# A transformer-like graph kernel in f32: one weight tile moved into the attention, one half of the layer norm's statistics moved behind the queries' products

## The chip, the cores and the metric

The kernel runs on one core of a Trainium2 chip. The metric is the device time of one execution, in microseconds (us). A core has five engines, which work side by side and wait for each other through semaphores: TensorE (PE in the profile) multiplies matrices into PSUM; VectorE (DVE) and ScalarE (ACT) do elementwise work; GpSimd (POOL) does a little of it and issues some transfers; SyncE (SP) issues most transfers. Each engine takes its own instructions strictly in the order in which the kernel wrote them.

## The reference, cut to what matters

`x` is 16 batches of 1024 nodes with 256 channels. Everything is f32.

```python
# layer 0
h = relu(layernorm(x))
c = mean of h over the channels              # one number a node
A = abs(abs(sigmoid(c_m - c_n) - 0.5) - 0.5) * 2, symmetrised
g = einsum('bcn,bnm->bcm', h^T, adj * A)     # graph sums
q = relu(g * para)^T                         # 4 heads of 64
k, v = split(h @ kv_w)
x = x + softmax(q k^T * scale) v
# layer 1
h = relu(layernorm(x))
agg = einsum('nm,bmd->bnd', A_hat, h)        # A_hat from adj
z = relu(batchnorm(agg @ W1.T + b1))
x = x + batchnorm(z @ W2.T + b2)
```

The weights `adj * A` are made from `1 - tanh(abs(c_m - c_n) / 2)`, for eight tiles of 128 nodes a batch.

## The kernel before

The batches are pipelined. While the attention of batch b runs, the weights of batch b+1 are begun. Then come the graph sums and the queries, keys and values of b+1 (`graph_seven`), then the first linear part of layer 1 of batch b (`linear1_all`), then the attention of b+1. One such cycle repeats for b = 1 to 14; batch 0 and 1 have a start of their own, and the last batches and the second linear layer with its batch norm stand at the end. Inside the main part the order of every engine is the order of the lines in the program (`manual_schedule`), so a step that is moved in the code moves in its engine's queue.

**The attention** (`attention`) has four steps for a batch, each for half of the queries and one pair of heads. `scores` (L797) makes eight tiles: PE multiplies keys by queries into one of three PSUM tiles of `ps_s` (L803), ACT takes the exp (L811), DVE adds the exps up (L817, L823, L826). Behind the eighth tile come the steps in `before_last` (L829), then the last addition (L831), then the steps in `after_last` (L832). `partial` turns and reduces the sums on DVE (L839, L847), `values` multiplies the exps by the values on PE (L855) and turns the result on DVE (L868). In the third step ACT also runs `collect` (L882) and `spread` (L897) for the first half's reciprocals.

**The weight tiles** are hung on these steps by `hooks` (run in `before_last`) and `aside` (run in `after_last`), L1449 to L1456. `differences` (L350) makes Abs (L353) and Tanh (L356) on ACT. What is left, subtracting one and multiplying by `adj`, is done in one of two ways: `masked` (L370) with one DVE instruction, or `masked_aside` (L359) with a small memset on DVE (L363), which ACT waits for, an Identity on ACT (L365) and a product on POOL (L366). `weights` (L344) is `differences` and `masked` together. Before, tiles 0 to 3 are made in steps 0 to 3 of the attention with `masked_aside`; tiles 4 to 7 are made in `graph_seven` with `masked`.

**The graph sums** (`graph_seven`, from L509) multiply a matrix of 2 x 2 blocks with seven products in place of eight (a Strassen form, in Winograd's order). The products `m1` to `m_7` go to PSUM: one accumulator `x` that ACT copies out three times (L631, L655, L659), `m7`, and the two tiles `gps[0]` and `gps[1]`. DVE makes the sums of weight tiles (`make_t1` to `make_t4`: L557, L560, L553, L565). At the end DVE joins the parts: L662, L673, L675 and L676 add PSUM to the copies in `room`; L667 to L671 make sums of `hT` for the keys and values.

**Values and keys** (`Seven`, from L684) have the same form of seven products each. All copies of the accumulator run on ACT (L727), all additions on DVE (L730), and products 6, 5 and 3 go on in the accumulator only after the copy ahead of them. The values' products are L717 on PE, the keys' L712. Between them stand the queries' products with `para` (L742), `add1` (the second half of the attention's result is added to `x`, L931), the store of `x` (`leave`) and the load of the next (`arrive`), both on SP's queue.

**The layer norm of layer 1** (`Norm`): `stats` is eight instructions for four node tiles (L253 four times, L255 four times, DVE), `invert` an addition on DVE (L259) and a power on POOL (L260), `shifts` one DVE instruction that waits for the power (L266), `relu` one ACT instruction a node tile (L281). Before, `stats`, `invert` and `shifts` of tiles 0 to 3 stand among the joining additions of the graph sums (L660, L661, L672), their relus among the values' products (L735, L740); those of tiles 4 to 7 stand behind `add1` (L752, L753, L762), with relus among the keys' products (L774, L779). The first products of the linear layer (L1018) read the relus of tiles 0 to 3.

POOL also issues half of the sixteen small transfers that lay out the attention's result (L923); SP issues the other half.

## Time and profile before

| | |
|---|---|
| median of 3 runs | 2389.51 us (2387.36 to 2390.91) |
| the profiled execution | 2388.5 us, its span 2386.6 us |
| instructions | 25696 |
| mean granted clock of TensorE | 0.995 |
| exps (L811, ACT) | 512, 477.4 us busy |
| scores (L803, PE) | 2048 records, 457.3 us busy |
| masks on DVE (L370) | 71, 84.0 us busy, 1217 ns each |
| masks on POOL (L366) | 56, 132.3 us busy, 2362 ns each |

The span is what the profiler saw from the first to the last instruction; the execution's own time has 1.9 us around it. A line of the timeline gives the start in us, the duration, the engine, the line of the kernel, the operation, the tiles written and read, the shapes and the count; in square brackets stand the idle time of the engine ahead of it and what ended it. PE's records overlap, since matmuls are pipelined, so their starts are read. One f32 matmul of 512 columns leaves two records. "V" below is the start of the first values' product of a cycle.

### The profile page before, as it was taken

Reading aid. Unit: us, or ns where it says so; the run is one execution under the profiler, and the core shown is the slowest. Engines: PE = TensorE matmul, PEld = TensorE weight load, DVE = VectorE, ACT = ScalarE, POOL = GpSimd, SP = SyncE. Lnnn points to the kernel's source line nnn. Section 1 sums busy time; section 2 is a strip of 40 time slices with the busy share of each in tenths; the row PEclk is TensorE's granted clock in tenths of the full one; section 3 lists DMA queues with packets and bytes.
Section 4 is the critical chain, followed back from the end, with each engine's and each line's share of the span. In section 5 each row is a group of like instructions: output and inputs, shape, how many; then the busy total and the mean of one; then the engine's idle time right before and its main releaser. Section 6 shows DMA issues by size and latency. Waiting matters only on the chain.

```text
span 2386.6 us, 25696 instructions
## 1 busy us (share of the span) xinstructions
PE 2341.1 (98%) x8258; PEld 1031.6 (43%) x8258; DVE 1977.9 (83%) x2922; ACT 1418.5 (59%) x2058; POOL 444.2 (19%) x565
## 2 busy tenths in 40 slices
PE   8999999999999999999999999999999999999995
PEld 4443444434343434444343434344443434444444
DVE  6888989897988889897979898897979798757766
ACT  6846556473847465565748375656656575446654
POOL 3041212122212112121122211121212121100000
PEclk9999999999999999999999999999999999999998
DMA  5043343523342434435233424243353421355569
GB/s 194 10 141 97 133 141 115 159 106 115 105 145 82 172 98 135 139 115 159 106 119 123 142 71 168 94 166 108 125 149 112 133 100 54 109 207 187 175 239 380
DMA packets 167264, 323.78 MB, mean 136 GB/s; under 512 B 33616, under 2 KB 100688, under 8 KB 167120
## 3 DMA queue, kind: packets, MB, share of 16 engines
q1 hardware_dynamic: 143696, 266.44, 32.7%
q0 software_dynamic: 18816, 38.83, 6.0%
q10 hardware_dynamic: 4608, 16.78, 1.7%
q8 instruction: 67, 1.10, 0.2%
q14 instruction: 77, 0.63, 0.1%
HBM read 202.38 MB, written 100.72 MB: 127 GB/s over the span
## 4 chain that ended last, share of the span: by engine, by line
PE 63%; DVE 20%; issue 6%; ACT 5%; POOL 4%; DMA 1%; DVEq 0%; SPq 0%; ACTq 0%; POOLq 0%
PE f_aps L1018 16%; PE f_s L803 11%; PE f_o L855 11%; PE f_zps L1125 6%; PE f_zx L1672 4%; ACT f_p L811 4%; PE f_zm L1672 3%; DVE f_w L370 3%; POOL f_att L923 2%; PE f_kpsx L712 2%; DVE f_w L557 2%; DVE f_sums L826 2%; PE f_kps L712 2%; DVE f_sums L839 1%; DVE f_v L553 1%
## 5 line engine op out<-in xcount | busy, mean ns | idle before, releaser
L811 ACT ACTIVATE f_p<-f_s 128x1024 f32<-128x1024 f32 x512 | 477.4, 1046 | 89.1 <-PE f_s L803 88.9
L803 PE MATMUL f_s<-f_qT,f_kT 64*128 64x512 f32 x2048 | 457.3, 596 | 0.5 <-issue 0.5
L855 PE MATMUL f_o<-f_p,f_v 128*64 128x512 f32 x2048 | 453.6, 595 | 0.0
L803 PEld LDWEIGHTS f_s<-f_qT,f_kT 64*128 64x128 f32 x2048 | 191.1, 186 | 264.2 <-issue 117.7
L855 PEld LDWEIGHTS f_o<-f_p,f_v 128*64 128x64 f32 x2048 | 141.4, 137 | 304.3 <-issue 265.1
L366 POOL TENSOR_TENSOR f_w<-f_w,f_adj 128x1024 f32<-128x1024 f32 x56 | 132.3, 2362 | 700.7 <-ACT f_w L365 565.2
L923 POOL DMA_DIRECT2D f_att<-f_oT x256 | 136.7, 541 | 398.3 <-DVE f_oT L906 391.4
L826 DVE TENSOR_TENSOR f_acc<-f_acc,f_p 128x1024 f32<-128x1024 f32 x128 | 155.9, 1218 | 4.5 <-ACT f_p L811 4.5
L826 DVE TENSOR_TENSOR f_sums<-f_sums,f_p 128x1024 f32<-128x1024 f32 x128 | 155.8, 1217 | 0.0
L353 ACT ACTIVATE f_w<-f_row,f_col 128x1024 f32<-128x1024 f32 x127 | 147.0, 1157 | 13.7 <-DMA f_row<-frow 10.3
L356 ACT ACTIVATE f_w<-f_w 128x1024 f32<-128x1024 f32 x127 | 134.4, 1058 | 4.0
L817 DVE TENSOR_TENSOR f_acc<-f_p,f_p 128x1024 f32<-128x1024 f32 x64 | 78.5, 1226 | 56.3 <-ACT f_p L811 56.3
L1018 PE MATMUL f_aps<-f_ahatT,f_hs 128*128 128x512 f32 x256 | 115.1, 592 | 0.0
L1018 PE MATMUL f_aps<-f_ahatT,f_h_b 128*128 128x512 f32 x256 | 112.7, 593 | 0.1
L1018 PE MATMUL f_aps<-f_t,f_hs 128*128 128x512 f32 x256 | 112.5, 592 | 0.0
L572 PE MATMUL f_gps<-f_w,f_h_a 128*128 128x512 f32 x224 | 111.0, 598 | 0.0
L365 ACT ACTIVATE f_w<-f_w,f_now 128x1024 f32<-128x1024 f32 x56 | 64.3, 1149 | 75.3 <-DVE f_now L363 75.2
L281 ACT ACTIVATE f_h_a<-f_x,f_shift_a,f_rstd_a 128x256 f32<-128x256 f32 x126 | 73.8, 587 | 37.2 <-DVE f_shift_a L266 37.2
L281 ACT ACTIVATE f_h_b<-f_x,f_shift_b,f_rstd_b 128x256 f32<-128x256 f32 x128 | 69.3, 595 | 43.9 <-DVE f_shift_b L266 43.9
L823 DVE TENSOR_TENSOR f_sums<-f_p,f_p 128x1024 f32<-128x1024 f32 x64 | 78.1, 1221 | 20.5 <-ACT f_p L811 20.4
L370 DVE SCALAR_TENSOR_TENSOR f_w<-f_w,f_adj 128x1024 f32<-128x1024 f32 x71 | 84.0, 1217 | 4.2 <-ACT f_w L356 4.2
L1148 ACT ACTIVATE f_z<-f_zps,f_b 128x512 f32<-128x512 f32 x60 | 38.0, 684 | 75.2 <-PE f_zps L1125 75.2
(292 smaller groups left out, 3982.6 us busy)
## 6 DMA issues: line engine op xcount, KB each, us to landing
f_t<-ft SPq DMA_DIRECT2D x84, 512.0 KB, 9.9
fz<-f_z SPq DMA_DIRECT2D x64, 512.0 KB, 9.8
f_x<-in_x_dram SPq DMA_DIRECT2D x31, 1024.0 KB, 7.9
f_zb<-fz SPq DMA_DIRECT2D x42, 512.0 KB, 4.6
fx<-f_x SPq DMA_DIRECT2D x16, 1024.0 KB, 4.4
fgs<-f_gs POOLq DMA_DIRECT2D x28, 512.0 KB, 3.0
fhT<-f_hQ POOLq DMA_DIRECT2D x112, 128.0 KB, 3.2
f_hT<-fhT SPq DMA_DIRECT2D x28, 512.0 KB, 6.3
```

What stands on the lines that cost most here:

```text
L281: nc.scalar.activation(self.h[:, c, :], self.xt[:, c, :], AF.Relu, bias=self.shift[:, c : c + 1], scale=self.rstd[:, c : c + 1], accum_out ...
L353: nc.scalar.activation(w, rows[b], AF.Abs, bias=cols[b][:, c : c + 1], scale=0.5 / C)
L356: nc.scalar.activation(w, w, AF.Tanh)
L370: nc.vector.scalar_tensor_tensor(w, w, 1.0, adj_t[c], ALU.subtract, ALU.mult)
L803: nc.tensor.matmul(ps[:, e, :], kT[rows_e, pair, ts(m, P)], qT[rows_e, pair, ts(g, 512)], start=True, stop=True,)
L811: nc.scalar.activation(p, ps, AF.Exp)
L826: nc.vector.tensor_add(to, to, p)
L855: nc.tensor.matmul(o_of[s][e * HD : (e + 1) * HD, :], v[:, m, ts(2 * pair + e, HD)], p[:, e, :], start=(m == 0), stop=(m == NC - 1),)
L923: queue.dma_start(t[ts(j, 32), :, a].rearrange("r h c i -> r h (c i)"), oT[ts(a, 32), :, j].rearrange("r h c i -> r h (c i)"),)
L1018: nc.tensor.matmul(ps, left[:, m, :], right(m), start=not more and m == 0, stop=(m == KH - 1), skip_group_check=more,)
L1125: nc.tensor.matmul(ps[i], left[:, ts(i, P)], right, start=not more, stop=True, skip_group_check=more,)
L1672: nc.tensor.matmul(ps, left[:, m, :], right[:, m, :], start=start and m == 0, stop=(m == 1), skip_group_check=not start,)
```

## The change

Three things are changed, in all fourteen cycles.

- Tiles 0, 2, 3 and 4 are made in steps 0 to 3 of the attention with `masked_aside`, and tile 1 in step 1 as well, with `weights`, whose DVE instruction stands ahead of L831. `graph_seven` makes tiles 5 to 7 only.
- `stats`, `invert` and `shifts` of the first half are moved from the end of the graph sums behind `add1`, around two of the values' additions; their four relus move from among the values' copies to among the keys' copies. The last addition from `gps[1]` (L676) moves ahead of the sums of `hT`.
- `gps[1]` is allocated ahead of `gps[0]`.

```diff
-            gps = [ps_s.tile([P, N], F32, tag="s", name=f"f_gps_{b}_{d}") for d in range(CC)]
+            gps = {
+                d: ps_s.tile([P, N], F32, tag="s", name=f"f_gps_{b}_{d}") for d in reversed(range(CC))
+            }
             add0, collect, invert, spread, scale, add1 = left
-            for c in range(4):
-                assert (b, c) in ws
-            w4th = w4.tile([P, N], F32, tag="w4", name=f"f_w_{b}_4")
...
-            differences(b, 4, w4th)
             differences(b, 5, w5th)
...
-            masked(b, 4)
             masked(b, 5)
...
             nc.scalar.copy(room[:, 1], x)
-            norm.stats(0, 4)
-            norm.invert(0, 4)
             nc.vector.tensor_add(room[:, 2], room[:, 2], m7)
+            nc.vector.tensor_add(room[:, 2], room[:, 2], gps[1][:, 0:512])
...
             nc.vector.tensor_sub(kt4, part(1, 0), kt2)
-            norm.shifts(0, 4)
             nc.vector.tensor_add(room[:, 3], room[:, 1], m7)
             both = lambda d: room[:, 2 * d : 2 * d + 2].rearrange("p n k -> p (n k)")
             nc.vector.tensor_add(both(0), both(0), gps[0])
-            nc.vector.tensor_add(room[:, 2], room[:, 2], gps[1][:, 0:512])
...
             V.copy(0, 0)
-            norm.relu(0, 2, False)
             V.product(2)
...
             V.copy(1, 0)
-            norm.relu(2, 4, False)
...
             load_more(2, 3)
+            norm.stats(0, 4)
+            norm.invert(0, 4)
             V.add(1, 0, 7)
             V.add(1, 1, 7)
+            norm.shifts(0, 4)
             norm.stats(4, NC)
             norm.invert(4, NC)
...
             K.copy(0, 0)
+            norm.relu(0, 2, False)
             K.product(2)
             norm.shifts(4, NC)
             K.add(0, 0, 2)
             K.product(6)
             K.copy(1, 0)
+            norm.relu(2, 4, False)
...
                 if b + 1 < B:
-                    for c in range(2 if b == 0 else 4):
-                        if b == 0:
+                    if b == 0:
+                        for c in range(2):
                             hooks.setdefault(c, []).append(lambda c=c: weights(b + 1, c))
-                            continue
-                        hooks.setdefault(c, []).append(lambda c=c: differences(b + 1, c))
-                        aside[c] = [lambda c=c: masked_aside(b + 1, c)]
+                    else:
+                        for i, c in enumerate((0, 2, 3, 4)):
+                            hooks.setdefault(i, []).append(lambda c=c: differences(b + 1, c))
+                            aside[i] = [lambda c=c: masked_aside(b + 1, c)]
+                        hooks[1].append(lambda: weights(b + 1, 1))
```

## The prediction, made before the changed kernel ran

> **What bounds the kernel now.** I read the page's busy times first, then the starts of the matmuls in order of time, then who waited for whom, then ACT, DVE and POOL in one cycle.

> ```profile
> PE 2341.1 (98%) x8258; PEld 1031.6 (43%) x8258; DVE 1977.9 (83%) x2922; ACT 1418.5 (59%) x2058; POOL 444.2 (19%) x565
> ```

> PE sets the time; a stall counts only where PE's next matmul starts late. The cycle of a batch lasts 130.2 to 130.3 us in 11 of the 13 full cycles (130.6 and 134.3 in the others), and the matmuls' starts cut it: graph sums 24.58, values' products 6.88, keys' products 6.31 (so 13.19 for both), linear layer 36.15, attention 56.34. A 512-column f32 matmul record follows the last after 0.429 us where nothing waits (linear layer: 56 records in 24.03). So the graph sums hold 0.55 us of waiting and the products about 1.1: more than that times 14 cycles can't be won there. What the engines beside PE do between the first product (806.51) and the linear layer (819.70):

> ```profile
> 804.61 0.68 DVE L662 TENSOR_TENSOR f_kT<-f_kT,f_gps 128x512 f32<-128x512 f32 x1
> 808.75 0.16 DVE L266 SCALAR_TENSOR_TENSOR f_shift_b<-f_mv_b,f_rstd_b 128x4 f32<-128x4 f32 x1 [0.93 <-POOL f_rstd_b L260]
> 808.83 0.68 DVE L673 TENSOR_TENSOR f_kT<-f_kT,f_gps 128x512 f32<-128x512 f32 x1
> 811.88 2.35 DVE L742 TENSOR_TENSOR f_qT<-f_kT,f_qT 128x1024 f32<-128x1024 f32 x2
> 814.15 1.22 DVE L931 TENSOR_TENSOR f_x<-f_x,f_att 128x1024 f32<-128x1024 f32 x1
> 815.29 1.28 DVE L730 TENSOR_TENSOR f_v<-f_v,f_vps 128x512 f32<-128x512 f32 x2
> 816.49 1.40 DVE L253 BATCH_NORM_STATS2 f_st_b<-f_x 128x6 f32<-128x256 f32 x4
> 817.80 0.36 DVE L255 BATCH_NORM_AGGREGATE f_mv_b<-f_st_b 128x2 f32<-128x6 f32 x4
> 818.20 0.17 DVE L259 TENSOR_SCALAR f_var_b<-f_mv_b 128x4 f32<-128x4 f32 x1
> 818.44 1.01 POOL L260 TENSOR_TENSOR f_rstd_b<-f_var_b,f_mhalf 128x4 f32<-128x4 f32 x1 [9.72 <-DVE f_var_b L259]
> 819.49 0.17 DVE L266 SCALAR_TENSOR_TENSOR f_shift_b<-f_mv_b,f_rstd_b 128x4 f32<-128x4 f32 x1 [0.53 <-POOL f_rstd_b L260]
> 819.69 1.09 ACT L281 ACTIVATE f_h_b<-f_x,f_shift_b,f_rstd_b 128x256 f32<-128x256 f32 x2 [1.00 <-DVE f_shift_b L266]
> ```

> DVE is one unbroken row of work here; the first shifts (808.75) wait for POOL. From the end of the statistics' additions (L259, 818.20) it takes 1.29 us through POOL to the shifts, and 0.20 more to the relu. PE's keys hang on ACT's copies:

> ```profile
> 816.30 0.59 ACT L727 COPY f_kT<-f_kpsx 128x512 f32<-128x512 f32 x1 [1.22 <-PE f_kpsx L712]
> 816.96 1.10 PE L712 MATMUL f_kpsx<-f_hT,f_kvs 128*128 128x512 f32 x2
> ```

> Copy start to next product start: 0.66.

> **Part one: the first half's statistics go behind the queries' products.** Out of the graph sums' end go four L253, four L255, L259, the wait for POOL and L266. They come back after L931, but the relus that need the shifts now stand in ACT's queue *ahead* of the keys' copies: copy, relu 0-1, copy, relu 2-3. Count from the first values' product (V = 806.51). DVE, start to start as in the rows: L662 starts when the copy L655 is done, V-3.5; L676 (moved up) 0.70 later, since it adds to the same tile; the four hT sums end at V+0.4. L673 waits for the copy L659 (0.20 to 0.79): V+0.85, where it stood at V+2.32. L675 0.72 later; 1.14 for it; 0.60 for V.add; L742 twice 1.13; L931 1.14; with 0.06 for the dependence the statistics start at V+6.78. L253 1.32, L255 0.40, L259 0.08, then two V.adds. POOL's power starts 0.25 after L259 (V+8.50) and takes 1.01; shifts at V+9.79; relu at V+9.99. The pair of relus holds ACT 1.00 us (808.95 to 809.95 before), so the second keys' copy starts at V+10.99 and the product behind it at V+11.65. Before it stood at 816.96 = V+10.45: **1.20 us later**. From there to the linear layer it is 2.74 as before: relu 2-3 ends before the next copy's data (1.14 after the product), so it is hidden, and the relus 4-5 stand behind the third copy with shifts ready by V+13.1.
> What the values win ahead of that is eaten: L673 frees the bank of product 7 at V+1.5 (before: V+3.0, PE stood 0.36), and copy (1,0) no longer stands behind two relus (809.95), so the keys' products start near V+6.5 instead of V+6.88; but PE then stands some 1.5 us at the fifth product. Bounds: 0.9 (DVE gaps of 0.60 where I took 0.70 to 1.14 for two of them, and no relu overhead) to 1.45 (POOL's power at the 1.24 of the first half's row, L260 at 807.48). I take 1.20. POOL has nothing else at that time: its eight attention issues ran 803.20 to 807.47. SP sees its store of x1 behind L931 some 2 us sooner, which nothing waits for.

> There is one gift. In the fourth cycle the values' products took 10.92 instead of 6.88: POOL's issues of f_att paused for 2.65 us, the power came late, L266 with DVE behind it 3.39 late, and PE stood 2.63. After the change the power is asked for at V+8.5, so such a pause is covered: **-4.0 us once** (0 if the pause falls elsewhere).

> [...]

> **Part two: the fifth weight tile in the attention.** The graph sums lose an Abs, a Tanh and a masked product (L370, 1.13 apart). Two of their products wait for L370 (0.09 and 0.27 us beyond 0.429), both behind three L370 in a row; with one fewer both masks are ready in time: **-0.36** (bounds 0 and -0.55, all the waiting there). In exchange the second attention step gets Abs, Tanh and L370 of tile 1. The rows of that step and the next:

> ```profile
> 879.60 1.06 ACT L356 ACTIVATE f_w<-f_w 128x1024 f32<-128x1024 f32 x1
> 882.05 1.15 ACT L365 ACTIVATE f_w<-f_w,f_now 128x1024 f32<-128x1024 f32 x1 [1.40 <-DVE f_now L363]
> 885.19 5.61 ACT L811 ACTIVATE f_p<-f_s 128x1024 f32<-128x1024 f32 x6 [1.99 <-PE f_s L803]
> 880.71 1.22 DVE L831 TENSOR_TENSOR f_acc<-f_acc,f_sums 128x1024 f32<-128x1024 f32 x1
> 881.88 0.06 DVE L363 MEMSET f_now<- 128x1 f32 x1
> 884.02 7.14 PE L803 MATMUL f_s<-f_qT,f_kT 64*128 64x512 f32 x32
> ```

> ACT seems to have room (1.40 + 1.99 idle against 2.2 of work), but the room is cut up by DVE. Tanh of tile 2 ends at 880.66, so tile 1's Abs and Tanh end at 882.9. L370 stands in DVE's queue ahead of L831 and the memset, and waits for that Tanh: 882.93; L831 1.14 later, 884.07; memset 1.17 later, 885.24; Identity (L365) 0.17 later, 885.41, which holds ACT 1.06. The first exp of the third step starts at 886.47 instead of 885.19: 1.28 late. PE has three PSUM tiles of scores: its fourth tile needs the first exp's end, 887.49, against its own 886.70, and ACT's exps (0.907 apart) outrun PE's tiles (0.86) no more, so the eighth tile starts at 891.22 instead of 890.13. **+1.10 a cycle** (bounds 0.8, the fourth tile's delay alone, and 1.28, the whole delay of the exp). It ends there: the next Identity ends at 900.0, before that step's first scores at 900.4. DVE is 3.4 us late at its o transpose (L868), but the PSUM tile that this frees is wanted at 892.

> **Part three: the PSUM order.** Values' product 4 and the keys' x take the tiles of the sums. Now L675 and L676 free both by 811.4, and product 4 starts at 811.56 with no wait but the last product; after, both are free by V+2.8, 2 us before it. Worth 0 either way; if the allocation ignores the order, also 0.

> **The sum.** 14 cycles have the change: 14 x (1.20 - 0.36 + 1.10) = 27.2; less 4.0 = 23.1 us. The profiled execution took 2388.5 us (span 2386.6 and 1.9 around it), so 2411.6; the median of the runs is 1.0 above it: **2412.6**. From the bounds: 14 x (0.9 - 0.55 + 0.8) - 4.0 = 12.1, so 2401.6; 14 x (1.45 + 1.28) = 38.2, so 2427.7.

> **Rivals.**
> - *Both costs are covered* (faster). The shifts would have to be ready when the keys' first copy ends, V+8.1, 1.7 us before my sum, and ACT's late exp would have to be absorbed. Then the products gain the 0.41 of the earlier keys and the sums 0.36: 14 x 0.77 + 4.0 = 14.8, so 2374.7. For it: DVE does lose its wait for POOL (0.93) early on. Against: the statistics, 1.9 us, come back into the same row of DVE work ahead of the two V.adds. It decides from a DVE that is 1.7 us earlier. 5%.
> - *Only the keys' wait shows*; the attention absorbs the tile: 14 x 0.84 - 4.0 = 7.8, so 2397.3. For it: the idle times of ACT. Against: they lie on both sides of the DVE wait. 9%.
> - *Only the attention's wait shows*: 14 x (1.10 - 0.77) - 4.0 = 0.6, so 2390.1. Against: as the first. 3%.
> - *The gaps bring the clock down* in each cycle: 3.41 us at half clock lose up to 1.4 beyond the gap, as the fourth cycle shows (4.03 - 2.63): 14 x 1.4 = 20 more, 2432. [...] 5%.

> **How the numbers follow.** My sum holds 78%. The range 2401 to 2426 is its own bounds, with the top cut a little since not all bounds fall the same way; the rival at 2397 is just outside. Told from no change are 0.2%, 4.8 us: faster 5%, same 3%, slower 92%.

> **What would show it.** In the changed profile: the products' stretch at 14.4 us instead of 13.19 with the wait of f_kpsx for the copy L727 over 1.5 us once a cycle, and ACT's relu of f_h_b waiting 1.8 us for the shifts between the keys' copies; the attention at 57.4, all of the growth in its third step; the sums near 24.2; 132.2 a cycle. I am wrong if the relu finds its shifts ready, or if the third step's exps start on time.

## The result, and the profile after

The changed kernel takes **2410.36 us** (median of 6 runs, 2409.34 to 2411.0) against 2390.15 us before (6 runs, 2387.36 to 2391.0): ratio 1.0086, 95% interval 1.0073 to 1.0099. It is slower by some 20 us. The profiled execution took 2410.24 us, its span 2408.4, the mean granted clock 0.995 as before.

The starts of PE's first matmuls cut a cycle into stages. The table has the median over the 14 cycles and, in the last column, how much the sum over the 14 grew:

| stage | before, us | after, us | sum over 14 cycles, us |
|---|---|---|---|
| graph sums | 24.58 | 24.22 | -5.1 |
| values' products | 6.89, longest 10.92 | 6.39, longest 6.39 | -11.0 |
| keys' products | 6.31 | 7.96 | +22.9 |
| linear layer | 36.14 | 36.14 | 0 |
| scores of the third attention step | 7.07 | 8.04 | +13.6 |
| whole cycle | 130.26 | 132.02 | +20.3 |

The sum, 20.3 us, is nearly the whole growth of the span (2386.6 to 2408.4, 21.8); the rest lies ahead of the first cycle and behind the last attention. All other steps of the attention are as before, within 0.2 us over the 14 cycles. The cycle with the long values' products (10.92) is the third of the 14; the prediction and some expectations call it the fourth.

The first line of the page's busy times hardly tells the two kernels apart:

```profile
PE 2342.4 (97%) x8258; PEld 1029.5 (43%) x8258; DVE 1987.1 (83%) x2922; ACT 1418.0 (59%) x2058; POOL 440.6 (18%) x565
```

The waits of PE do. Two rows of the changed kernel (engine, tile and line, what it waited for, then us in total, number of times, longest):

```profile
PE f_kpsx L706 <- ACT f_kT L721: 20.9, 14, 1.8
...
PE f_s L800 <- ACT f_p L808: 6.7, 14, 0.5
```

In the kernel before, the one row of this kind that came once a cycle was another, a values' product waiting for a sum of DVE:

```profile
PE f_vps L717 <- DVE f_kT L673: 4.8, 14, 2.6
```

It is gone after the change. Both new waits come exactly 14 times, once a cycle: a keys' product waits for ACT's copy, and a tile of scores waits for an exp. (Line numbers of the changed kernel are smaller by 3 to 8: the copies are L721, which were L727, the scores L800, the exps L808.)

The timeline of the changed kernel from the queries' products to the linear layer, in the same cycle as before, in which V is 811.02:

```profile
814.30 2.35 DVE L734 TENSOR_TENSOR f_qT<-f_kT,f_qT 128x1024 f32<-128x1024 f32 x2
816.57 1.22 DVE L928 TENSOR_TENSOR f_x<-f_x,f_att 128x1024 f32<-128x1024 f32 x1
817.71 1.40 DVE L253 BATCH_NORM_STATS2 f_st_b<-f_x 128x6 f32<-128x256 f32 x4
819.42 0.17 DVE L259 TENSOR_SCALAR f_var_b<-f_mv_b 128x4 f32<-128x4 f32 x1
820.80 0.16 DVE L266 SCALAR_TENSOR_TENSOR f_shift_b<-f_mv_b,f_rstd_b 128x4 f32<-128x4 f32 x1
...
818.52 0.59 ACT L721 COPY f_kT<-f_kpsx 128x512 f32<-128x512 f32 x1 [0.32 <-DVE f_st_b L253]
821.00 1.09 ACT L281 ACTIVATE f_h_b<-f_x,f_shift_b,f_rstd_b 128x256 f32<-128x256 f32 x2 [1.90 <-DVE f_shift_b L266]
822.00 0.56 ACT L721 COPY f_kT<-f_kpsx 128x512 f32<-128x512 f32 x1
...
820.12 1.02 PE L706 MATMUL f_kps<-f_kt,f_kvs 128*128 128x512 f32 x2
822.61 1.12 PE L706 MATMUL f_kpsx<-f_hT,f_kvs 128*128 128x512 f32 x2 [1.47 <-ACT f_kT L721]
```

Read it from below. PE's product at 822.61 stands 1.47 us for the copy at 822.00. ACT could have made that copy a good 1.5 us sooner, but ahead of it in the queue stands the relu at 821.00, and ACT stands 1.90 us for the shifts (820.80), which came out of the statistics that now begin only behind `add1`. The relu's own reader, the linear layer, starts at 825.38 and is in no hurry. What is lost is lost by the copy *behind* the relu.

The timeline of the changed kernel from the second attention step to the third, whose scores start at 889.69:

```profile
885.26 1.06 ACT L356 ACTIVATE f_w<-f_w 128x1024 f32<-128x1024 f32 x1
887.39 1.06 ACT L356 ACTIVATE f_w<-f_w 128x1024 f32<-128x1024 f32 x1
890.90 1.15 ACT L365 ACTIVATE f_w<-f_w,f_now 128x1024 f32<-128x1024 f32 x1 [2.45 <-DVE f_now L363]
891.96 5.57 ACT L808 ACTIVATE f_p<-f_s 128x1024 f32<-128x1024 f32 x6
...
888.48 1.23 DVE L370 SCALAR_TENSOR_TENSOR f_w<-f_w,f_adj 128x1024 f32<-128x1024 f32 x1 [2.13 <-ACT f_w L356]
889.63 1.22 DVE L828 TENSOR_TENSOR f_acc<-f_acc,f_sums 128x1024 f32<-128x1024 f32 x1
890.79 0.06 DVE L363 MEMSET f_now<- 128x1 f32 x1
...
889.69 2.85 PE L800 MATMUL f_s<-f_qT,f_kT 64*128 64x512 f32 x12
893.01 4.78 PE L800 MATMUL f_s<-f_qT,f_kT 64*128 64x512 f32 x20 [0.48 <-ACT f_p L808]
```

Here a DVE instruction stands ahead of its time. L370 waits 2.13 us for the second Tanh; the addition L828 and the memset L363 have to stand behind it; ACT's Identity waits 2.45 us for that memset; and the first exp of the third step stands behind the Identity. It starts 2.27 us after the step's first scores, where it was 1.17 before. PE makes three tiles of scores (12 records of the 32) and stands 0.48 us. Its 13th record starts 3.32 us after the first, where 12 records at the pace of a 7.07 us step take 2.65, and the other 20 take 0.30 longer than at that pace: the 0.97 by which the step grew.

### The profile page after: what moved, and what is told of

Read it like the earlier page. It is cut to its first block, busy times and chain, and to the rows that moved or that the text cites. A ratio compares the mean times of both kernels' runs of the same rounds, so it can differ in the third digit from the quotient of the medians.

```text
span 2408.4 us, 25710 instructions
## 1 busy us (share of the span) xinstructions
PE 2342.4 (97%) x8258; PEld 1029.5 (43%) x8258; DVE 1987.1 (83%) x2922; ACT 1418.0 (59%) x2058; POOL 440.6 (18%) x565
## 4 chain that ended last, share of the span: by engine, by line
PE 77%; ACT 10%; DVE 8%; issue 2%; DMA 1%; POOL 1%; DVEq 0%; SPq 0%; ACTq 0%; POOLq 0%
PE f_aps L1015 16%; PE f_o L852 14%; PE f_s L800 14%; PE f_gps L571 7%; PE f_zps L1122 6%; PE f_gpsx L571 6%; ACT f_p L808 5%; PE f_zx L1671 4%; PE f_zm L1671 3%; ACT f_w L356 1%; ACT f_w L353 1%; PE f_kpsx L706 1%; PE f_gps L413 1%; DVE f_st_b L253 1%; PE f_z2ps L1609 1%
## 5 line engine op out<-in xcount | busy, mean ns | idle before, releaser
L808 ACT ACTIVATE f_p<-f_s 128x1024 f32<-128x1024 f32 x512 | 476.8, 1046 | 60.3 <-PE f_s L800 60.3
L800 PE MATMUL f_s<-f_qT,f_kT 64*128 64x512 f32 x2048 | 463.7, 600 | 6.7 <-ACT f_p L808 6.7
L800 PEld LDWEIGHTS f_s<-f_qT,f_kT 64*128 64x128 f32 x2048 | 185.7, 185 | 282.2 <-ACT f_p L808 140.9
L356 ACT ACTIVATE f_w<-f_w 128x1024 f32<-128x1024 f32 x127 | 134.4, 1058 | 4.1
L365 ACT ACTIVATE f_w<-f_w,f_now 128x1024 f32<-128x1024 f32 x56 | 64.4, 1150 | 93.5 <-DVE f_now L363 93.5
L370 DVE SCALAR_TENSOR_TENSOR f_w<-f_w,f_adj 128x1024 f32<-128x1024 f32 x71 | 85.3, 1219 | 33.7 <-ACT f_w L356 33.7
L814 DVE TENSOR_TENSOR f_acc<-f_p,f_p 128x1024 f32<-128x1024 f32 x64 | 84.9, 1327 | 27.9 <-ACT f_p L808 27.9
L281 ACT ACTIVATE f_h_a<-f_x,f_shift_a,f_rstd_a 128x256 f32<-128x256 f32 x126 | 73.9, 587 | 38.3 <-DVE f_shift_a L266 38.3
L281 ACT ACTIVATE f_h_b<-f_x,f_shift_b,f_rstd_b 128x256 f32<-128x256 f32 x128 | 69.2, 595 | 45.5 <-DVE f_shift_b L266 45.5
```

Of the source, the lines that this page charges most:

```text
L281: nc.scalar.activation(self.h[:, c, :], self.xt[:, c, :], AF.Relu, bias=self.shift[:, c : c + 1], scale=self.rstd[:, c : c + 1], accum_out ...
L356: nc.scalar.activation(w, w, AF.Tanh)
L800: nc.tensor.matmul(ps[:, e, :], kT[rows_e, pair, ts(m, P)], qT[rows_e, pair, ts(g, 512)], start=True, stop=True,)
L808: nc.scalar.activation(p, ps, AF.Exp)
```

## The experiments

Stages are named as in the table above. Line numbers differ by a few from kernel to kernel.

### Each wait taken out of the changed kernel

**e1.** The mask of tile 1 is moved behind the last addition and the memset of its step; Abs and Tanh stay.

```diff
-                        hooks[1].append(lambda: weights(b + 1, 1))
+                        hooks[1].append(lambda: differences(b + 1, 1))
+                        aside[1].append(lambda: masked(b + 1, 1))
```

> The changed kernel, with the DVE mask of tile 1 put behind the memset that tile 2's Identity waits for; ACT's work is the same. My theory (the mask stands ahead of the memset in DVE's queue and waits for a Tanh): tile 1's Tanh ends 1.24 us before the third step's scores start, the Identity follows at once, the exps start on time; the third step's scores take 7.07 us again in place of 8.04, so 14 x 0.97 = 13.6 us less than 2410.4: about 2396.8. Rival (ACT has too much work in that step, wherever the mask stands): 8.04 stays, 2410.

2396.26 us against 2389.35 before: 1.0027 (1.0018 to 1.0037), so 14.1 below the changed kernel. The third step's scores are back at 7.07 us in every cycle, keys stay at 7.96. The timeline of e1 at the same place:

```profile
881.84 1.06 ACT L356 ACTIVATE f_w<-f_w 128x1024 f32<-128x1024 f32 x1
882.81 1.13 ACT L365 ACTIVATE f_w<-f_w,f_now 128x1024 f32<-128x1024 f32 x1
885.31 5.61 ACT L808 ACTIVATE f_p<-f_s 128x1024 f32<-128x1024 f32 x6 [1.37 <-PE f_s L800]
...
882.00 0.06 DVE L363 MEMSET f_now<- 128x1 f32 x1
882.93 1.23 DVE L370 SCALAR_TENSOR_TENSOR f_w<-f_w,f_adj 128x1024 f32<-128x1024 f32 x1 [0.87 <-ACT f_w L356]
```

The memset now stands ahead of the mask, the Identity follows the Tanh with no idle time, and the exps wait for PE (1.37) rather than PE for them. The same three instructions, with the same work, cost nothing in this order: the price was the wait in DVE's queue, not ACT's 2.2 us of Abs and Tanh.

**e2.** The two pairs of relus are moved one copy back in ACT's queue; statistics and shifts stay late.

```diff
             K.copy(0, 0)
-            norm.relu(0, 2, False)
...
             K.copy(1, 0)
-            norm.relu(2, 4, False)
+            norm.relu(0, 2, False)
...
             K.copy(1, 1)
+            norm.relu(2, 4, False)
```

> The changed kernel, with each pair of relus of the first half one copy later in ACT's queue (behind the second and third keys' copy instead of the first and second). The statistics stay where the change put them. My theory (the second copy stands behind a relu whose shifts are late): the second copy runs at V+9.3, the product behind it at V+10.0 instead of V+11.6, the linear layer starts at V+12.7 instead of V+14.35: 14 x 1.62 = 22.7 us less, about 2387.7. Rival (the relus' 2.0 us of ACT time among the copies are what stretches the keys): V+14.3 stays within 0.3, 2406 to 2410.

2388.18 us: 0.9995 (0.9986 to 1.0004), 22.2 below the changed kernel. Keys are back at 6.31, the third step stays at 8.05. ACT's rows in e2, the second copy and the first pair of relus:

```profile
813.21 0.59 ACT L721 COPY f_kT<-f_kpsx 128x512 f32<-128x512 f32 x1 [1.22 <-PE f_kpsx L706]
813.89 1.09 ACT L281 ACTIVATE f_h_b<-f_x,f_shift_b,f_rstd_b 128x256 f32<-128x256 f32 x2
```

The copy waits for PE's product again, as it did before the change, and the relu finds its shifts ready. The late statistics cost next to nothing as such: the keys' products of all 14 cycles take 89.5 us, where they took 89.0 before the change.

**e3.** Both edits together.

> Both edits at once (mask behind the memset, relus one copy later). If the two waits are separate, as my theory has it: 2410.4 - 13.6 - 22.7 = 2374.1 us, some 16 us faster than the kernel before. If one hides the other, the gain is less than the sum of the two edits' own gains.

2374.48 us against 2389.35 before: 0.9932 (0.9918 to 0.9945). The two gains, 14.1 and 22.2, add up to 36.3; measured together they are 35.9. So the two waits are separate, and with both gone the change is what it leaves: shorter sums, shorter values, no pause, and a kernel faster than the one before.

**e4.** The other way to undo the keys' wait: the relus stay where the change put them, and the statistics move ahead of the queries' products and `add1`.

```diff
             V.add(0, 0, 2)
+            norm.stats(0, 4)
+            norm.invert(0, 4)
...
+            norm.shifts(0, 4)
             add1()
...
-            norm.stats(0, 4)
-            norm.invert(0, 4)
             V.add(1, 0, 7)
             V.add(1, 1, 7)
-            norm.shifts(0, 4)
```

> The changed kernel, with the first half's statistics ahead of the queries' products and their shifts ahead of the addition of the attention's result; the relus stay among the keys' copies where the change put them. My theory (the lateness of the shifts is the price, not the place of the relus): shifts at V+7.3 instead of V+9.8, the first pair of relus runs behind the first copy without a wait, the linear layer starts near V+12.7: 14 x 1.6 = 22 us less, about 2388. Rival (the relus' ACT time among the copies): V+14.3 stays, 2410.

2393.29 us: 1.0014 (1.0005 to 1.0023). That is 17 below the changed kernel, but 5 more than expected: keys came to 6.45, in four cycles to 6.8, instead of 6.31, and the linear layer to 36.25 instead of 36.14. Rows of e4's timeline in another cycle show where it comes from:

```profile
943.39 0.15 DVE L266 SCALAR_TENSOR_TENSOR f_shift_b<-f_mv_b,f_rstd_b 128x4 f32<-128x4 f32 x1
944.02 1.23 DVE L928 TENSOR_TENSOR f_x<-f_x,f_att 128x1024 f32<-128x1024 f32 x1 [0.48 <-issue]
948.15 0.68 DVE L724 TENSOR_TENSOR f_v<-f_v,f_vps 128x512 f32<-128x512 f32 x1
...
948.88 3.70 PE L1015 MATMUL f_aps<-f_ahatT,f_h_b 128*128 128x512 f32 x8
```

DVE stands 0.48 us ahead of `add1` (L928) with nothing to wait for but its own issue: eight instructions that wait for the sixteen small transfers stand there. In the trace of the changed kernel each of the eight starts 0.07 to 0.10 us after the last (813.83 to 814.49). There, where they come while a values' addition (0.68 us) and the first queries' product (L734, 1.22 us) run, DVE has no idle time ahead of `add1`; behind the short L266 (0.15 us) it has. DVE is so late that the values' addition L724 ends just as PE wants the PSUM tile it frees for the linear layer, and in four cycles later than that (PE's row of waits: 1.3 us in 4 times). So the cause of the keys' wait is confirmed a second way. Against e2 the keys lost 3.5 us over the 14 cycles and the linear layer 1.4; by my estimate the first comes mostly from these eight instructions, which I had not counted; the second was not followed up.

### Each part put alone into the kernel before

**e5.** Only the five weight tiles, with the mask where the change has it.

> The kernel before, with the five weight tiles in the attention alone. My theory: attention +0.97, graph sums -0.36 a cycle, values and keys as before (13.19): 14 x 0.61 = 8.5 us more than before, about 2398.6. Rival (the lateness at the attention only shows together with the moved statistics): 2385, the gain of the graph sums alone.

2391.94 us: 1.0008 (0.9999 to 1.0017). I was 6.7 us off. The third step is 8.04 and the sums 24.22, as expected, but values fell too, from 6.89 to 6.39 (longest 8.72), which I had put down to the other part. The timeline of e5, in which V is 806.65:

```profile
807.01 1.24 POOL L260 TENSOR_TENSOR f_rstd_b<-f_var_b,f_mhalf 128x4 f32<-128x4 f32 x1
808.29 0.16 DVE L266 SCALAR_TENSOR_TENSOR f_shift_b<-f_mv_b,f_rstd_b 128x4 f32<-128x4 f32 x1 [0.93 <-POOL f_rstd_b L260]
```

The shifts still make DVE wait 0.93 us for POOL, but at V+1.64 instead of V+2.24, since with one mask fewer DVE and then POOL come to everything some 0.6 us sooner. That is enough for the sum that PE's product 7 waits for (e10 below moves POOL's power alone). Per cycle: +0.97 - 0.36 - 0.49 = +0.12, and 14 times that is 1.7 us; the stages in question grew by 1.1, of which 0.7 is one longer second step of the attention.

**e6.** Only the statistics, their relus and L676.

> The kernel before, with the moved statistics and relus alone (and L676 moved up). My theory: values' and keys' products 14.35 instead of 13.19, the rest as before: 14 x 1.16 = 16.2 us more, less up to 4.0 us if a pause of POOL's issues cost the kernel before that much: 2402 to 2406. No cycle's values' products should be longer than 6.5 us. Rival (the statistics' absence from the end of the graph sums shortens these): graph sums under 24.4, total under 2400.

2402.15 us: 1.005 (1.0036 to 1.0063). Keys 7.96, values 6.395 and never above 6.40, sums 24.58: as expected. The stages of e5 grew by 1.1 and those of e6 by 11.8, of both together by 20.3. The difference, 7.4 us, is the values' gain of about 8 us, which each part brings alone and which can be had only once, less the 0.7 of e5's one longer step.

**e7.** Only the order of the two PSUM tiles.

> The kernel before, with the two PSUM tiles of the graph sums in the other order alone. My theory: nothing waits for either, so 2390 within 2 us, and every stage keeps its length to 0.05 us. Rival (product 4 of the values waits for the tile): the values' products shorter or longer by 0.1 us or more a cycle.

2389.6 us: 0.9999 (0.999 to 1.0008). Values 6.88 with the longest at 10.84: nothing is changed.

### What the parts are worth without their waits

**e8.** e5 with the mask behind the memset, as in e1. Statistics and relus are where they were before the change.

> The kernel before, with the five weight tiles in the attention and the mask of tile 1 behind the memset; statistics and PSUM order as before. The tiles alone shortened the values' products from 6.88 to 6.39, which I had not counted for them. Theory: that gain comes from the graph sums' shorter DVE row (L906, POOL's issues and its power all sooner), so it stays here: graph sums 24.22, values 6.39, keys 6.31, third step's scores 7.07; 14 x (0.36 + 0.49) = 11.9 us less than before and some 1.7 us less of POOL's pause: about 2375.8. Rival (the values gained only because the attention's step was late): values 6.88 again, about 2384.

2376.58 us: 0.9948 (0.9935 to 0.9962). Values 6.39, but 10.19 in the third cycle. The tile in the attention, its mask in the right place, brings most of what there is to gain; the move of the statistics adds little to it (2374.48 in e3). In the values' products it adds 4.2 us over the 14 cycles, 3.8 of them in the one cycle in which a pause of POOL (2.66 us) holds its power.

**e9.** In the kernel before, the attention's second half is scaled ahead of `add0`, so that POOL could issue its transfers sooner.

```diff
-                add0()
...
+                add0()
```

> The kernel before, with two neighbours on DVE in the graph sums exchanged: the scaling of the attention's result (L906), which POOL's eight transfers wait for, ahead of the addition of the first half (L931). Nothing else is changed and no work is added or taken. Theory (the first half's shifts wait for the power, which stands behind those transfers in POOL's queue): the transfers start 1.14 us sooner, the power with them, values 6.39 in place of 6.88: 14 x 0.49 = 6.9 us less than before, and some 1 to 2 us less of POOL's pause: about 2381. Rival (DVE's own row sets the values): 6.88 stays, 2389.

2389.0 us: 0.9996 (0.9987 to 1.0005). A miss: values came to 6.83, not 6.39. The row of POOL in e9:

```profile
803.35 4.25 POOL L923 DMA_DIRECT2D f_att<-f_oT  x8 [19.15 <-DVE f_x L931]
```

POOL's transfers wait for L931, which is `add0`: it reads the same buffer (`f_att`) that they write. My forecast had missed this second condition: with scale and addition exchanged the transfers start at V-3.49 (V is 806.84 in e9), against V-3.31 before, not 1.14 us sooner.

**e10.** In the kernel before, SP issues twelve of the sixteen transfers instead of eight.

```diff
-                            queue = nc.sync if a < 2 else nc.gpsimd
+                            queue = nc.sync if a < 3 else nc.gpsimd
```

> The kernel before, with twelve of the sixteen small transfers of the attention's result issued by SP and four by POOL, in place of eight and eight; no work on DVE, ACT or PE is moved. (In the kernel with the scaling first, POOL's transfers started no sooner, since they also wait for L931, which reads the one buffer of f_att; so that run did not move POOL's power.) Theory: the power stands behind four issues, 2.1 us sooner, the first half's shifts no longer hold L673, values 6.39 in place of 6.88, and POOL's pause in the fourth cycle costs less or nothing: 14 x 0.49 = 6.9 and up to 4.0 us less: 2378 to 2383. Rival (DVE's own row or ACT's relus set the values): 6.8 to 6.9 stays, 2389.

2380.19 us: 0.9959 (0.9946 to 0.9973). Values are 6.39 in all cycles, the long one too. This tells why the values were long before: POOL's power stood behind POOL's own issues, and four fewer of them are enough. The sums grew in some cycles (347.0 over 14, from 344.4); e11 shows where.

**e11.** e8 with the edit of e10.

> Five tiles in the attention with the mask behind the memset (2376.6), and twelve transfers issued by SP. Theory: values 6.39 in every cycle, the fourth's 10.19 gone: about 4 us less, 2372.5, the fastest of the kernels here. If SP's longer row makes the addition of the second half late, keys' products grow beyond 6.31 and it is not below 2376.

2377.43 us: 0.9952 (0.9939 to 0.9966), not the 2372.5 I expected. The sums grew by 5.7 over the 14 cycles against e8 (339.1 to 344.8). The waits of PE in one such stretch of e11:

```profile
PE f_gps L569 <- DMA f_gs<-fgs: 1.1, 1, 1.1
```

PE's waits for this load come to 3.4 us in e11, and to as much in e10. The load of the graph sums' operand stands behind the first half's transfers on SP's queue, and there are now twelve of them there instead of eight.

**e12.** e8, with the four extra transfers on SP only for the second half (`g` is 1), which no such load follows.

```diff
-                            queue = nc.sync if a < 2 else nc.gpsimd
+                            queue = nc.sync if a < 2 + g else nc.gpsimd
```

> Five tiles in the attention with the mask behind the memset, and twelve transfers on SP for the second half of the queries only; the first half's stay eight and eight. In the run with twelve for both, the graph sums grew by 5.6 us in all, since PE waited for the load of f_gs, which stands behind the first half's transfers in SP's queue. Theory: graph sums 24.22 again, values 6.39 in every cycle: 2376.6 less 4.2 = 2372.4. If the load is late because of anything else, the graph sums stay above 24.4 and the time at 2376 or more.

**2371.93 us** (2369.59 to 2372.42): 0.9927 (0.9914 to 0.9941), the fastest of all here. Sums 24.22, values 6.39 in every cycle, keys 6.31, third step 7.07: each stage at the shortest that any run here shows.

## Why the prediction was right

The forecast was 2412.6 us, the median is 2410.36, and the cases it was made of held.

- **Keys and values, +1.20 a cycle: measured +1.15** (13.20 to 14.35). The chain came as worked out: shifts at V+9.78 (forecast V+9.79), relu V+9.98 (V+9.99), copy V+10.98 (V+10.99), product V+11.59 (V+11.65). A little of this closeness is luck: the statistics began 0.09 us sooner than forecast (817.71, V+6.69), and from L259 to the shifts it took 1.38 us instead of 1.29. e2 and e4 show that it is this chain: without the wait in ACT's queue, by either way, the stall goes.
- **Graph sums, -0.36: measured -0.36.** e5 and e8 show it with the tiles alone.
- **Attention, +1.10: measured +0.97.** The mechanism is the one foretold, and e1 confirms it; the size was a little off. The first exp came 1.10 us late instead of 1.28, mostly since the second Tanh follows the first after 2.13 us (885.26 to 887.39) where I had added up 2.24.
- **The pause, -4.0 once: covered.** Values are 6.39 at their longest, and e6 shows that the late statistics do it (6.40 at the longest there, 8.72 with the tiles alone in e5). The pause itself came all the same (2.66 us, ahead of 547.84).
- **PSUM order, 0:** e7.
- **The rivals.** e1 is what the second looks like (2396.26, forecast 2397.3), and e2 what the third looks like (2388.18, forecast 2390.1), so they had the right prices for what didn't happen. The granted clock stayed at 1.0 behind all 14 new gaps, 13 of 1.47 us and one of 1.75, so the fourth is out too. The first, both costs covered, forecast 2374.7, is e3 (2374.48).

The weak step was hidden in a sum. I laid all the values' gain (0.38 a cycle in the forecast, 0.49 measured) to the moved statistics. e5 shows that the weight tile brings it alone, by making POOL's power earlier. For the whole change the sum is the same; for a part taken out of it, it is off by about 7 us, as e5's forecast was. Where one wait has two possible cures in the same change, neither price is told by the whole.

## What to carry to other kernels

Idle time on an engine was no room here where another engine ended it (ACT's 2.45 us ahead of its Identity, ended by DVE's memset, and its 1.90 us ahead of the relu, ended by the shifts): ask what stands *behind* the new instruction in its queue, and when its input is ready. Both losses here came from an instruction that waited ahead of work which was ready (a relu ahead of a copy, a mask ahead of an addition and a memset), and both went when it was moved behind that work, with no work taken away. When a change bundles parts, measure them apart as well as together: here two parts cured the same wait, and a third cure lay in the transfers of a queue that neither touched (e10).

## What the runs showed of the hardware

**POOL paused at the same three of its transfers.** In the kernel before and in the changed one, issues 129, 250 and 371 of POOL's transfers, 121 apart, came after an idle time of 2.65 to 2.72 us that no wait in the profile ends. They start at 543.48, 1167.49 and 1760.27 us before and at 547.84, 1178.04 and 1778.41 after the change, so in these two kernels the pause came at the same issues and not at the same times. e5 and e8 have it in the third cycle too (2.67 and 2.66 us). The rows of the kernel before in that cycle:

```profile
543.48 2.12 POOL L923 DMA_DIRECT2D f_att<-f_oT  x4 [2.65 <-issue]
545.62 1.03 POOL L260 TENSOR_TENSOR f_rstd_b<-f_var_b,f_mhalf 128x4 f32<-128x4 f32 x1
546.68 0.16 DVE L266 SCALAR_TENSOR_TENSOR f_shift_b<-f_mv_b,f_rstd_b 128x4 f32<-128x4 f32 x1 [3.39 <-POOL f_rstd_b L260]
```

and of the changed kernel:

```profile
547.84 2.10 POOL L920 DMA_DIRECT2D f_att<-f_oT  x4 [2.66 <-issue]
555.69 1.03 POOL L260 TENSOR_TENSOR f_rstd_b<-f_var_b,f_mhalf 128x4 f32<-128x4 f32 x1 [5.74 <-DVE f_var_b L259]
```

The same pause, but the power is now asked for long after it, and nobody waits. In e11, which issues fewer on POOL, the last three issues ahead of the power run from 535.80 us in this cycle, and the power starts behind them at 537.41 with no idle time. What makes POOL pause was not tried.

**A short stand of PE brought the clock down, or did not.** e8's rows of PE in the third cycle:

```profile
544.93 1.16 PE L712 MATMUL f_vps<-f_kvs,f_kt 128*128 128x128 f32 x8 [1.89 <-DVE f_kT L668]
547.34 1.91 PE L712 MATMUL f_vps<-f_kvw,f_kt 128*128 128x128 f32 x8
```

and those of e5:

```profile
548.27 1.16 PE L712 MATMUL f_vps<-f_kvs,f_kt 128*128 128x128 f32 x8 [2.00 <-DVE f_kT L668]
550.26 1.06 PE L712 MATMUL f_vps<-f_kvw,f_kt 128*128 128x128 f32 x8
```

After a stand of 1.89 us the same group of eight took 1.91 us in e8, at half clock for 3.41 us; after 2.00 us it took 1.06 in e5, at full clock. The longest values' stage was 10.19 us in e8 and 8.72 in e5. In the kernel before, the clock fell to 0.5 for 3.41 us (548.50 to 551.91) after the stand of 2.63 us and stayed at 1.0 after one of 2.01 us (from 2322.01). So in these runs the length of a stand alone did not decide, and the one of 2.01 us gives no safe bound.

```profile
543.05:546.46 3.41, 1.53 (x12) 1.50 (x13) 2.31 (x4) 2.14 (x5) 1.03 (x1) 1.00 0.08 19
546.46:549.87 3.41, 3.41 (x18) 3.41 (x17) 3.41 (x5) 1.00 (x2) 0.00 (x0) 0.50 0.00 0
...
544.47:547.88 3.41, 1.79 (x16) 1.60 (x15) 0.43 (x2) 0.81 (x2) 2.93 (x5) 1.00 0.22 49
547.88:551.29 3.41, 3.02 (x25) 2.99 (x26) 3.38 (x5) 2.92 (x6) 0.00 (x0) 1.00 0.00 0
```

e8's stand lies in one window, so that PE is busy for 1.53 us of it, and the next window runs at half clock. e5's stand is cut in two by the end of a window, and the clock stays. The windows of the kernel before and of the changed one agree: of those at full clock, all 6 in which PE stood for 2.14 us or more were followed by one at half clock, and none of the 1377 others, in which it stood for 1.75 us at most (by the records' modelled ends). The 2.01 us gap in the kernel before was cut in two as well, into 1.43 and 0.59 us. So was one of 2.02 us in the changed kernel (from 2342.74), into 0.75 and 1.27, but with a second gap PE stood for 2.14 us of the later window (2343.49 to 2346.90), and the next ran at half clock. The 14 new gaps of 1.47 to 1.75 us, some whole in a window and some cut, left the clock at 1.0.

**Eight waits in a row took DVE's time behind a short instruction.** Ahead of `add1` they left DVE idle for 0.48 us where they came behind an instruction of 0.15 us (e4, at 944.02), in another cycle 0.83 (at 813.42), and for none in the kernel before and the changed one, where they come while instructions of 0.68 and 1.22 us run. Why the other cycle took longer was not tried.
